# The state scan of a selective-scan mixer: 13 of 64 input products on ScalarE and GpSimd, convolutions summed in PSUM, seams and head in a new order

## The chip, the cores and the metric

The kernel runs on one core of a Trainium2 chip. Five engines share the work: TensorE (PE, with weight loads as PEld), VectorE (DVE), ScalarE (ACT), GpSimd (POOL) and SyncE (SP, which here only issues DMAs). Each has its own instruction stream; semaphores order them against each other. The metric is the device time of one execution in microseconds (us), as the median of the runs.

## The reference, cut to what matters

The model has two layers on an image x of shape (2, 256, 64, 64). The first layer is an area attention and an LSTM; they are not touched. The second layer begins with "the mixers", and ends with a mixture of experts, which is not touched either. The mixers take a normalised x and add to each of five groups of channels something else: 128 channels pass through, three groups of 32 channels get a depthwise convolution (3x3, 1x11, 11x1), and the last 32 channels get a selective scan over the 4096 pixels of an image:

```python
o_hw = _dwconv2d(x_hw, w_hw, b_hw, [(1, 1), (1, 1)])
o_w = _dwconv2d(x_w_, w_w, b_w, [(0, 0), (5, 5)])
o_h = _dwconv2d(x_h_, w_h, b_h, [(5, 5), (0, 0)])
o_m = _mamba(x_mb, ...)
...
# _mamba, with D_INNER = 64 and D_STATE = 16
u = jax.nn.silu(causal_conv1d(xm) + conv1d_b)
delta = jax.nn.softplus(jnp.einsum('blr,dr->bld', dt, dt_proj_w) + dt_proj_b)
A = -jnp.exp(A_log)
dA = jnp.exp(delta[..., None] * A)
dBu = delta[..., None] * Bm[:, :, None, :] * u[..., None]
def step(h, inputs):
    dA_t, dBu_t, C_t = inputs
    h = h * dA_t + dBu_t
    y = jnp.sum(h * C_t[:, None, :], axis=-1)
    return (h, y)
...
y = y + u * D
y = y * jax.nn.silu(z)
out = jnp.einsum('bld,cd->blc', y, out_proj_w)
...
x = x + _L1_conv_ref(_ln_c(x), ...)
```

## The kernel before, in words

Two images times 64 inner channels fill the 128 partitions. The 4096 pixels are cut into four parts of 1024 columns, and each part is scanned for each of the 16 states: 64 steps in all, each on a 128x1024 tile. All of this is in the method `run`, under a manual schedule: the order in which the program text emits instructions is the order on each engine, and the framework adds only the semaphores.

One step (function `state`, with what the main loop emits around it) does this for part i and state n:
- `spread` (L1775): two matmuls in bf16 lay row n of B over all partitions, into a PSUM tile bn of two banks. It is emitted one step ahead.
- `decay` (L1770): ScalarE makes da = exp(delta * a_n), two steps ahead.
- the product (L1783): VectorE multiplies bn, in PSUM, by du = delta * u, in SBUF, in place.
- the scan (L1786): VectorE runs h = da * h + bn along the columns, da from SBUF and bn from PSUM, to hs in SBUF. hs has two buffers.
- `carry` (L1792): ScalarE keeps the last column for the next part.
- cs (L1793): GpSimd multiplies hs by the row of C, which a DMA (`bring`) has spread over the partitions two steps ahead.
- `add` (L1796): two steps later TensorE adds cs into yp, the PSUM tile of the part's sum over the states, by an identity matrix: four passes of f32. yp has one buffer of two banks. `skip` puts u * D into it first (at state 2 of a part).

Beside the steps, `beside` lists what else is done at which state, "early" ahead of the state's own instructions and "late" behind them:
- The next part's preparation: `line` (0), `line_out` (1), `inner` (half at 2, half at 3), `inner_out` with its Silu (4), `step_sizes` (5), `absolute` and `positive` (6), `exponent` (7), `logarithm` (8), then on GpSimd `lost`, `found`, `whole`, `times_u` and `b_third` (9 to 13, L1691, L1694, L1697, L1701 and L1656), which end in the next part's du, and the gate's Silu (13). Softplus is computed as max(v, 0) + ln(1 + exp(-|v|)), with a correction of the rounding of 1 + e, which needs the tiles e, top and wm.
- The end of the part before, the seam: `close` (L1807) multiplies yp by the gate on VectorE, behind state 1; `put` (L1818) projects it on TensorE into po, behind state 6; `put_out` (L1826) adds po to x on VectorE, ahead of state 7's product.
- The convolutions, in 14 pieces: band matrices multiply on TensorE into a PSUM bank "pc" or two; ScalarE copies each four channels to an SBUF tile `got` (L1454), and GpSimd adds them to x (L1456).

Banks of PSUM: bn takes four, yp two, and everything else shares the two banks with the tag "m".

Ahead of the scan stands the head (the first part's preparation, L1718 to L1752), with a pool of eight banks. There GpSimd does the remaining `add_norm`s (L1434), and VectorE and ScalarE share the softplus; `whole` is on VectorE, Ln reads 1 + e from wm, and the negative A (`a_neg`) is computed right after `inner_out`.

Of the kernel before, what the change touches and what calls it, by code (L numbers as in the profile page):

```python
# [10 lines left out]
F32 = mybir.dt.float32  # L11
# [1328 lines left out]
class Mixers:  # L1340
# [92 lines left out]
        part = self.sh.tok[:, w, :P]  # L1433
        eng.tensor_scalar(part, part, self.more[:, w : w + 1], self.less[:, w : w + 1], ALU.mult, ALU.add)  # L1434

    def convolutions(self, pool, ps):


        nc, xn, tok = self.tc.nc, self.xn, self.sh.tok
# [4 lines left out]
        def begin(at, n):  # L1444
            pc = bank("pc").rearrange("p (c w) -> p c w", w=WW)[:, :n]
            bias = self.b_conv[:, at : at + n].unsqueeze(2).to_broadcast([96, n, WW])
            nc.tensor.matmul(pc, self.ones, bias, start=True, stop=False, skip_group_check=True)
            return pc

        def end(at, pc):  # L1450

            for h in range(0, pc.shape[1], 4):
                got = pool.tile([P, 4, WW], F32, name="got", bufs=2)
                nc.scalar.copy(got, pc[:, h : h + 4])  # L1454
                to = tok[:, :, P + at + h : P + at + h + 4]
                nc.gpsimd.tensor_tensor(to, to, got.rearrange("p c w -> p w c"), ALU.add)  # L1456

        def fetch(name, at, n):
            t = pool.tile([P, 12 * WW], F32, name="band", bufs=2)[:, : n * WW]
# [15 lines left out]
        def turn(at):  # L1475
            pt = bank("pt").rearrange("p (i m) -> p i m", m=P)
            for c in range(8):
                h, i = divmod(c, 4)
                nc.tensor.matmul(
                    pt[64 * h : 64 * h + 64, i], xn[:, at + c, 1 : 1 + WW], self.sh.ident,  # L1480
                    start=True, stop=True, tile_position=(0, 64 * h),
                )
            turned = self.turned = pool.tile([P, 4, P], F32, name="turned")
            return lambda: nc.scalar.copy(turned, pt)

        def across(at, w):
# [57 lines left out]
    def run(self, left, check=None):  # L1544
# [5 lines left out]
        with ExitStack() as ctx:  # L1550
# [3 lines left out]
            ctx.enter_context(tc.manual_schedule())  # L1554
            nc.gpsimd.memset(self.carry, 0.0)
            psum, temps = [None], [pt]
            conv = self.convolutions(p1, lambda: psum[0])

            def bank(name):
                return psum[0].tile([P, 512], F32, name=name, tag="m")  # L1560
# [5 lines left out]
            def each_half(work):  # L1566
                for h in range(0, ML, 512):
                    work(slice(h, h + 512))
# [46 lines left out]
            def gate_out(now):  # L1615
                zs = now["zs"] = p1.tile([P, ML], F32, name="zs")
                each_half(lambda at: nc.scalar.activation(zs[:, at], now.pop(("pz", at.start)), AF.Silu))

            def inner(now, at):

# [5 lines left out]
            def inner_out(now):  # L1626
                u = now["u"] = p1.tile([P, ML], F32, name="u")
                each_half(
                    lambda at: nc.scalar.activation(u[:, at], now.pop(("pu", at.start)), AF.Silu, bias=sh.col("c1_b"))
                )  # L1630

            def b_and_c(now, at):

                pbc = now["pbc", at.start] = bank("pbc")
                nc.tensor.matmul(pbc, self.w_bc, now["u"][:, at], start=True, stop=True)
# [31 lines left out]
                    lambda at: nc.scalar.activation(e[:, at], now["pd", at.start], AF.Abs, bias=sh.col("dt_b"))  # L1667
                )

            def positive(now, at, apart):  # L1670
                pd = now.pop(("pd", at.start))
                if apart:
                    nc.vector.tensor_scalar(now["top"][:, at], pd, sh.col("dt_b"), 0.0, ALU.add, ALU.max)
                else:
                    nc.scalar.activation(now["top"][:, at], pd, AF.Relu, bias=sh.col("dt_b"))

            def exponent(now, add=True):
                now["wm"] = temp("wm")
# [1 line left out]
                if add:  # L1680
                    nc.scalar.activation(now["wm"], now["e"], AF.Identity, bias=self.unit[:, 0:1])

            def logarithm(now, less=False):
                wm = now["wm"]
                now["delta"] = p2.tile([P, ML], F32, name="delta")
                nc.scalar.activation(now["delta"], wm, AF.Ln)
                if less:
                    nc.scalar.activation(wm, wm, AF.Identity, bias=self.unit[:, 1:2])

            def lost(now, eng):  # L1690
                eng.tensor_tensor(now["e"], now["e"], now["wm"], ALU.subtract)  # L1691
# [14 lines left out]
            with ExitStack() as own:  # L1706
                pool = own.enter_context(tc.tile_pool(name="m_pre", bufs=1))
                psum[0] = own.enter_context(tc.tile_pool(name="m_psum_m", bufs=8, space=PSUM))
                temps.append(own.enter_context(tc.tile_pool(name="m_pre_t", bufs=1)))
                before_line(first, None)  # L1710
                pieces = self.centre(pool, 0, CN, nc.vector)
                others = self.centre(pool, CN, GC, nc.gpsimd)
                next(conv)
                for _ in range(3):
                    next(pieces)

                idle = pool.tile([P, 1], F32, name="idle")
                nc.scalar.activation(idle, sh.eps5, AF.Silu)  # L1718
                next(conv)
                next(conv)  # L1720
                next(pieces)
                next(others)
                next(others)
                line(first, 0)
                line_out(first, True)
                each_half(lambda at: inner(first, at))
                inner_out(first)
                nc.scalar.activation(self.a_neg, sh.prm[:, COL["A_log"]], AF.Exp)
                nc.gpsimd.tensor_scalar(self.a_neg, self.a_neg, -1.0, None, ALU.mult)
                for _ in others:  # L1730
                    pass
                for w in left:
                    self.add_norm(nc.gpsimd, w)
                each_half(lambda at: step_sizes(first, at))
                absolute(first)
                exponent(first, False)
                each_half(lambda at: positive(first, at, True))
                nc.vector.tensor_scalar(first["wm"], first["e"], 1.0, None, ALU.add)
                logarithm(first)
                each_half(lambda at: b_and_c(first, at))  # L1740
                b_first(first, nc.vector.tensor_copy)
                each_half(lambda at: b_rest(first, at))
                nc.vector.tensor_scalar(first["wm"], first["wm"], -1.0, None, ALU.add)
                lost(first, nc.vector)
                b_second(first)
                c_out(first, 0)
                found(first, nc.vector)
                whole(first, nc.vector)
                b_third(first, nc.vector)
                nc.scalar.activation(idle, sh.eps5, AF.Exp)  # L1750
                times_u(first, nc.vector)
                next(conv)  # L1752
                temps.pop()

# [1 line left out]
            p3 = ctx.enter_context(tc.tile_pool(name="m_3", bufs=2))  # L1756
            p4 = ctx.enter_context(tc.tile_pool(name="m_4", bufs=4))
            steps = [(i, n) for i in range(len(parts)) for n in range(DS)]
            checks = iter(()) if check is None else check(ps)

            def bring(i, n):
# [8 lines left out]
                nc.scalar.activation(da, parts[i]["delta"], AF.Exp, scale=self.a_neg[:, n : n + 1])  # L1770

            def spread(i, n):
                bn = parts[i]["bn", n] = ps.tile([P, ML], F32, name="bn")
                each_half(
                    lambda at: nc.tensor.matmul(  # L1775
                        bn[:, at], self.spread[:, n], parts[i]["b"][:, at], start=True, stop=True
                    )
                )

            def state(i, n):  # L1780
                now, end = parts[i], (i, n) == steps[-1]
                bn = now.pop(("bn", n))
                nc.vector.tensor_tensor(bn, now["du"], bn, ALU.mult)  # L1783
                hs = p3.tile([P, ML], F32, name="hs")
                carry = self.carry[:, n : n + 1]
                nc.vector.tensor_tensor_scan(hs, now.pop(("da", n)), bn, carry, ALU.mult, ALU.add)  # L1786
                if end:
# [40 lines left out]
            def beside(i, n):  # L1828
# [7 lines left out]
                if n in pieces:  # L1836
                    late.append(lambda: next(conv, None))
                if i > 0:
                    early += {7: [lambda: put_out(i - 1, 0, CN)]}.get(n, [])
                    late += {6: [lambda: put(i - 1, 0, CN)]}.get(n, [])  # L1840
                early += {13: [lambda: gate_out(now)]}.get(n, [])
                late += {12: [lambda: each_half(lambda at: gate(now, at))]}.get(n, [])
                if new is None:
# [2 lines left out]
                    return early, late  # L1846
                early += {
                    1: [lambda: line_out(new, False)], 4: [lambda: inner_out(new)],
                    6: [lambda: absolute(new), lambda: each_half(lambda at: positive(new, at, False))],
                    7: [lambda: exponent(new)], 8: [lambda: logarithm(new, True)],  # L1850
                    9: [lambda: lost(new, nc.gpsimd)],
                    10: [lambda: b_first(new, nc.scalar.copy), lambda: c_out(new, i + 1)]
                    + [lambda: found(new, nc.gpsimd)],
# [4 lines left out]
                }.get(n, [])  # L1858
                late += {
                    0: [lambda: before_line(new, now["xl"]), lambda: line(new, i + 1)],  # L1860
                    2: [lambda: inner(new, slice(0, 512))], 3: [lambda: inner(new, slice(512, ML))],
                    5: [lambda: each_half(lambda at: step_sizes(new, at))],
                    9: [lambda: each_half(lambda at: b_and_c(new, at))],
                }.get(n, [])
# [7 lines left out]
            for m, (i, n) in enumerate(steps):  # L1872
# [6 lines left out]
                    work()  # L1879
                state(i, n)  # L1880
                if n == 2 and i > 0:

                    skip(i)
                if m > 1:
                    each_half(lambda at: add(*steps[m - 2], at))
                if n == 1 and i > 0:
                    each_half(lambda at: close(i - 1, at))
                if m + 2 < len(steps):
                    bring(*steps[m + 2])
                for work in late:  # L1890
# [703 lines left out]
```

## Time and profile before

| what | us |
| --- | --- |
| median of three runs (2777.76, 2790.4, 2782.73) | 2782.73 |
| the profiled execution | 2774.13 |
| its span | 2772.3 |
| head of the mixers, to the first product of the scan | 1779.0 to 1813.3 of the span |
| scan, from there to the end of the last scan | to 2074.0 |
| last close, projection and sum | to 2082.1 |
| VectorE busy between 1813 and 2079 | 238.4 of 266.0 |

The profile is that of one execution, 8.6 us shorter than the median; the part of its time outside the span is 1.8 us. Groups of instructions are listed by line, engine, operation and tiles ("out<-in"), with busy time and the mean of one in ns. Lists of waits name the instruction that waited, what ended the wait, and then the us in total, the number of waits and the longest. A line with three durations shows the shortest, the median and the longest of a group.

### The profile page before, as it was taken

What the parts mean: (1) busy time and instruction counts of PE and PEld (TensorE: products, weight loads), DVE (VectorE), ACT (ScalarE), POOL (GpSimd) and SP (SyncE); (2) the same over time, 40 slices, a digit from 0 to 9 for tenths busy, and PEclk for the clock granted to TensorE, in tenths of its full rate; (3) what the DMA queues carried; (4) which work ended last, traced back from release to release, by engine and by line L of the source; (5) the groups of instructions that cost most, each with busy time, mean ns of one, the idle gap of its engine ahead of it and who ended that gap; (6) DMA issues with size and microseconds to landing.
All of it is one profiled execution on the core that took longest, in us unless ns stands there. A gap on an engine that the chain in (4) does not pass through costs nothing.

```text
span 2772.3 us, 45729 instructions
## 1 busy us (share of the span) xinstructions
PE 2576.4 (93%) x17021; PEld 1476.3 (53%) x17021; DVE 1903.3 (69%) x3670; ACT 1555.2 (56%) x2661; POOL 1258.9 (45%) x1214
## 2 busy tenths in 40 slices
PE   7999999999999999999999999878885999999984
PEld 2232333333333333332899999734443788888873
DVE  4787888888888888878666767798888422221116
ACT  2567677676767667666654555676637422222223
POOL 1354645453544554532341000288762366666651
PEclk9999999999999999999999999989998999999995
DMA  3566676777676767774450000055544366666648
GB/s 138 99 124 132 131 140 130 138 135 137 131 138 132 138 130 138 133 135 85 153 208 24 24 24 7 13 130 153 148 122 169 113 225 228 231 229 223 224 172 355
DMA packets 108923, 390.78 MB, mean 141 GB/s; under 512 B 19912, under 2 KB 24400, under 8 KB 98960
## 3 DMA queue, kind: packets, MB, share of 16 engines
q0 software_dynamic: 69184, 284.61, 43.1%
q1 hardware_dynamic: 38272, 98.87, 11.1%
q10 hardware_dynamic: 1232, 4.25, 0.4%
q8 instruction: 137, 2.24, 0.3%
q14 instruction: 98, 0.80, 0.1%
HBM read 178.81 MB, written 49.09 MB: 82 GB/s over the span
## 4 chain that ended last, share of the span: by engine, by line
PE 80%; DVE 10%; issue 4%; ACT 2%; DMA 2%; POOL 1%; SPq 0%; DVEq 0%; ACTq 0%; POOLq 0%
PE ps L302 11%; PE ph L2338 9%; PE av_o L416 9%; PE py L2350 8%; PE po L170 8%; PE ps L403 8%; PE z L906 7%; PE z L865 6%; PE ps L398 3%; DVE hs L1786 2%; PE yp L1796 2%; PE po L182 1%; PE po L416 1%; DVE more L318 1%; PE px L2324 1%
## 5 line engine op out<-in xcount | busy, mean ns | idle before, releaser
L372 DVE SCALAR_TENSOR_TENSOR acc<-vh,w_pe,acc 128x1008 f32<-128x1008 f32 (+7 forms) x384 | 476.5, 1244 | 8.4
L635 POOL DMA_DIRECT2D sx<-ex x304 | 264.7, 958 | 451.0 <-ACT ex L410 193.4
L410 ACT ACTIVATE ex<-ps 128x1024 f32<-128x1024 f32 x384 | 372.9, 1025 | 116.6 <-issue 56.8
L318 DVE CUSTOM_DVE_ANT_0 more<-ps,more 128x512 f32<-128x512 f32 x480 | 303.0, 687 | 133.4 <-PE ps L302 127.9
L2340 ACT ACTIVATE act<-ph,wt 128x256 f32<-128x256 f32 x272 | 128.9, 474 | 388.7 <-PE ph L2338 382.5
L2326 DVE COPY xt<-px 128x512 f32<-128x512 f32 x68 | 47.0, 692 | 390.7 <-PE px L2324 390.7
L2338 PE MATMUL ph<-xt,wt 128*128 128x256 f32 x1088 | 288.0, 387 | 0.0
L403 PE MATMUL ps<-q,k 32*128 32x512 f32 x2048 | 286.3, 602 | 0.0
L2350 PE MATMUL py<-wt,act 128*128 128x256 f32 x1088 | 278.9, 379 | 0.0
L314 ACT ACTIVATE more<-ps 128x1024 f32<-128x1024 f32 x240 | 233.5, 1029 | 16.8 <-ACT sx L410 5.9
L630 POOL TENSOR_TENSOR sx<-sx,ex 128x1024 f32<-128x1024 f32 x60 | 141.3, 2355 | 210.1 <-PE ps L302 168.9
L2338 PEld LDWEIGHTS ph<-xt,wt 128*128 128x128 f32 x1088 | 188.6, 189 | 60.1 <-DVE xt L2326 21.5
L2350 PEld LDWEIGHTS py<-wt,act 128*128 128x128 f32 x1088 | 201.8, 190 | 24.4
L416 PE MATMUL av_o<-ex,vt 128*32 128x512 f32 x1536 | 205.6, 606 | 0.0
L2365 POOL DMA_INDIRECT results<-y,ri x136 | 138.1, 1015 | 131.9 <-DVE y L2358 100.9
L874 ACT ACTIVATE t<-z,bias 128x128 f32<-128x128 f32 x440 | 127.9, 362 | 118.5 <-PE z L906 118.5
L302 PE MATMUL ps<-k,q 32*128 32x512 f32 x1088 | 183.3, 639 | 1.9 <-DVE nm L308 1.4
L865 PE MATMUL z<-xs,u 128*128 128x128 f32 x1536 | 181.9, 275 | 0.0
L865 PEld LDWEIGHTS z<-xs,u 128*128 128x128 f32 x1536 | 176.5, 192 | 0.3 <-ACT xs L1049 0.3
L1793 POOL TENSOR_TENSOR cs<-hs,cs 128x1024 f32<-128x1024 f32 x63 | 148.9, 2365 | 54.3 <-DVE hs L1786 31.3
L906 PE MATMUL z<-xs,v 128*128 128x128 f32 x1400 | 167.0, 275 | 0.2
L906 PEld LDWEIGHTS z<-xs,v 128*128 128x128 f32 x1400 | 162.5, 192 | 1.4 <-DVE xs L925 0.5
(477 smaller groups left out, 4661.1 us busy)
## 6 DMA issues: line engine op xcount, KB each, us to landing
sx<-ex POOLq DMA_DIRECT2D x304, 512.0 KB, 5.1
cs<-c_rows SPq DMA_DIRECT2D x128, 256.0 KB
y<-results SPq DMA_DIRECT2D x32, 512.0 KB
x<-xrows SPq DMA_DIRECT2D x8, 1024.0 KB
rows<-xt SPq DMA_DIRECT2D x16, 512.0 KB
out_x<-res POOLq DMA_DIRECT2D x15, 512.0 KB, 7.0
xrows<-xn SPq DMA_DIRECT2D x24, 256.0 KB
u_rows<-xs SPq DMA_DIRECT2D x14, 384.0 KB
```

Source lines behind the costliest of these rows:

```text
L302: made.append(nc.tensor.matmul(tiles[h // 2][:, h % 2], qs[G, i // HM][head(h), i % HM * P : (i % HM + 1) * P], keys[head(h)], start=True, ...
L314: nc.scalar.activation(held["more"][j], tiles[j], AF.Relu)
L318: nc.vector.tensor_tensor_reduce(more, tiles[h // 2][:, h % 2], more, -1.0, 3.0e38, ALU.add, ALU.min, accum_out=nms[G][:, 0, h, i : i + 1],)
L372: mark(nc.vector.scalar_tensor_tensor(part, vh[:, c, 2 + r0 + dy : 2 + r1 + dy, w0 + dx : w1 + dx], w_pe[:, c, k : k + 1], part, ALU.mult, ...
L403: nc.tensor.matmul(tiles[h // 2][:, h % 2], k[head(h), m % HM * P : (m % HM + 1) * P], qs[G, n][head(h)], start=False, stop=True, tile_pos ...
L410: nc.scalar.activation(exs[i], tiles[i], AF.Exp, scale=HD**-0.5)
L416: nc.tensor.matmul(to[head(h)], lhs, exs[h // 2][:, h % 2], start=first, stop=last, tile_position=(0, HD * h))
L635: nc.gpsimd.dma_start(total[i], exs[i], accum_op=ALU.add)
L865: nc.tensor.matmul(z[c][g], u[:, k, c, g], xin[j][:, k], start=g == GATES[0] and k == 0, stop=False, skip_group_check=True,)
L906: nc.tensor.matmul(z[c][g], v[:, k, c, g], h[:, k], start=False, stop=k == 1, skip_group_check=True,)
L2338: nc.tensor.matmul(ph[:, hc], wt[:, at : at + P], xt[:, c], start=c == 0, stop=c == 1)
L2350: nc.tensor.matmul(py[:, j], act[:, hc, j * P : j * P + P], wt[:, at : at + C], start=hc == 0, stop=hc == NH - 1,)
```

## The change

- **13 products leave VectorE.** In parts 0 to 2 for states 4, 6 and 15, in the last part for 4, 6, 9 and 15: TensorE spreads the row of B into two "m" banks (`spread_apart`, behind state 2, 4, 7 or 13), ScalarE copies both to an SBUF tile (top, wm or e, as they are free), and GpSimd multiplies it by du (`times_du`, ahead of state 3, 5, 8 or 14). On GpSimd this product stands ahead of the cs that the step of state 3, 5, 8 or 14 emits. The scan of these states reads da and this tile, both in SBUF.
- **Convolutions.** TensorE adds x itself to pc by an identity matrix, and ScalarE copies the sum straight to x; GpSimd's adds and the `got` tiles are gone.
- **Tables.** ln(1 + e) takes its 1 as the activation's bias and no longer reads wm; after each Silu the set that has both exp and ln is loaded.
- **Seams.** `close` goes behind state 2, right ahead of `skip`; `put_out` goes behind state 7; both halves of `inner` stand at state 3; hs has three buffers; `turned` uses the tile e.
- **Head.** ScalarE does abs, exp, ln and max in a row; `whole` is on GpSimd, and the add_norms are GpSimd's last; 12 small matmuls ("busy") stand ahead of `inner`.

```diff
         def begin(at, n):
...
             nc.tensor.matmul(pc, self.ones, bias, start=True, stop=False, skip_group_check=True)
+            before = tok[:, :, P + at : P + at + n].rearrange("p w c -> p c w")
+            nc.tensor.matmul(pc, self.sh.ident, before, start=False, stop=False, skip_group_check=True)
             return pc
 
         def end(at, pc):
-            for h in range(0, pc.shape[1], 4):
-                got = pool.tile([P, 4, WW], F32, name="got", bufs=2)
-                nc.scalar.copy(got, pc[:, h : h + 4])
-                to = tok[:, :, P + at + h : P + at + h + 4]
-                nc.gpsimd.tensor_tensor(to, to, got.rearrange("p c w -> p w c"), ALU.add)
+            n = pc.shape[1]
+            nc.scalar.copy(tok[:, :, P + at : P + at + n], pc.rearrange("p c w -> p w c"))
...
-            turned = self.turned = pool.tile([P, 4, P], F32, name="turned")
+            turned = self.turned = temp("e")[:, : 4 * P].rearrange("p (i m) -> p i m", m=P)
...
             def gate_out(now):
...
+                if now is not parts[-1]:
+                    nc.scalar.preload_act_table_set("natural_log_exp_and_others")
             def inner_out(now):
...
+                nc.scalar.preload_act_table_set("natural_log_exp_and_others")
...
-                nc.scalar.activation(now["delta"], wm, AF.Ln)
+                nc.scalar.activation(now["delta"], of, AF.Ln, bias=self.unit[:, 0:1])
...
+                busy = bank("busy")
+                for _ in range(12):
+                    nc.tensor.matmul(
+                        busy[:, :256], self.ones, self.spread[:, 0:2].rearrange("p n d -> p (n d)"), start=True, stop=True
+                    )
...
+            APART = {2: 4, 4: 6, 13: 15}, {2: 4, 4: 6, 7: 9, 13: 15}
+            NAMES = {4: "top", 6: "wm", 9: "top", 15: "e"}, {4: "top", 6: "wm", 9: "top", 15: "wm"}
...
+            def spread_apart(i, n):
+                banks = parts[i]["apart", n] = [bank("ba") for _ in range(2)]
+                for h, to in enumerate(banks):
+                    nc.tensor.matmul(
+                        to, self.spread[:, n], parts[i]["b"][:, 512 * h : 512 * h + 512], start=True, stop=True
+                    )
+            def times_du(i, n, name):
+                now = parts[i]
+                bn = now["bn", n] = temp(name)
+                for h, part in enumerate(now.pop(("apart", n))):
+                    nc.scalar.copy(bn[:, 512 * h : 512 * h + 512], part)
+                nc.gpsimd.tensor_tensor(bn, now["du"], bn, ALU.mult)
...
-                nc.vector.tensor_tensor(bn, now["du"], bn, ALU.mult)
-                hs = p3.tile([P, ML], F32, name="hs")
+                if n not in APART[i == last].values():
+                    nc.vector.tensor_tensor(bn, now["du"], bn, ALU.mult)
+                hs = p3.tile([P, ML], F32, name="hs", bufs=3)
...
-                    early += {7: [lambda: put_out(i - 1, 0, CN)]}.get(n, [])
+                    late = {7: [lambda: put_out(i - 1, 0, CN)]}.get(n, []) + late
+                if n - 1 in apart:
+                    s = apart[n - 1]
+                    early.append(lambda: times_du(i, s, NAMES[i == last][s]))
+                if n in apart:
+                    late.append(lambda: spread_apart(i, apart[n]))
...
-                    2: [lambda: inner(new, slice(0, 512))], 3: [lambda: inner(new, slice(512, ML))],
+                    3: [lambda: each_half(lambda at: inner(new, at))],
...
                 if n == 2 and i > 0:
+                    each_half(lambda at: close(i - 1, at))
                     skip(i)
                 if m > 1:
                     each_half(lambda at: add(*steps[m - 2], at))
-                if n == 1 and i > 0:
-                    each_half(lambda at: close(i - 1, at))
```

The head, as it is emitted behind `inner_out`, before and after:

```python
# before
a_neg; rest of the centring; add_norms (GpSimd); step_sizes; absolute; exponent; positive (VectorE)
wm = 1 + e (VectorE); logarithm of wm; b_and_c; b_first; b_rest; wm - 1; lost; b_second; c_out
found; whole (VectorE); b_third; times_u; next(conv)
# after
step_sizes; b_and_c; absolute; exponent; logarithm of 1 + e; positive (ScalarE)
rest of the centring; b_first; b_rest; c_out; a_neg; b_second; whole (GpSimd)
wm = (1 + e) - 1 (VectorE); lost; found; b_third; times_u; add_norms (GpSimd); next(conv)
```

## The prediction

> **What bounds the kernel now.** I read the page's chain first, then the table by stretches for the mixers (1779 to 2082 us of the span), then groups, waits and releases in there.
>
> ```profile
> PE 80%; DVE 10%; issue 4%; ACT 2%; DMA 2%; POOL 1%; SPq 0%; DVEq 0%; ACTq 0%; POOLq 0%
> ```
>
> The whole kernel is TensorE's, but the change lies only in the mixers, where the chain passes through VectorE (DVE). Three stretches by engine (us; busy PE, PEld, DVE, ACT, POOL with counts; granted clock; DMA share; GB/s):
>
> ```profile
> 1779.00:1813.00 34.00, 14.28 (x148) 8.73 (x149) 26.39 (x47) 20.84 (x33) 20.80 (x20) 0.71 0.09 28
> 1813.00:2079.00 266.00, 230.62 (x1474) 110.72 (x1473) 238.42 (x152) 160.19 (x238) 202.58 (x110) 0.97 0.54 143
> ```
>
> In the scan DVE is busy 238.4 of 266.0 us, PE 230.6, GpSimd (POOL) 202.6: three engines are nearly full, so work taken from DVE meets the next one soon. The groups (busy us, mean ns) and DVE's waits (us, times, longest):
>
> ```profile
> L1786 DVE TENSOR_TENSOR_SCAN hs<-da,carry,bn 128x1024 f32<-128x1024 f32 x64 | 150.2, 2347 | 13.9 <-POOL cs L1793 5.6 <-ACT da L1770 1.0
> L1783 DVE TENSOR_TENSOR bn<-du,bn 128x1024 f32<-128x1024 f32 x64 | 77.5, 1211 | 0.9 <-PE bn L1775 0.6
> ```
>
> ```profile
> DVE zs L1807 <- PE yp L1796: 6.0, 3, 3.0
> DVE hs L1786 <- POOL cs L1793: 5.6, 6, 1.2
> DVE x L1826 <- PE po L1818: 4.4, 3, 1.6
> DVE hs L1786 <- ACT da L1770: 1.0, 2, 0.5
> ```
>
> A state is a product and a scan. In undisturbed rows the scan starts 1.34 us after its product and the next product 2.26 us after the scan: 3.60 a state, set by DVE. POOL's product with C (L1793) repeats every 2.31 when nothing holds it.
>
> **What goes.** 13 products leave DVE: 13 x 1.34 = 17.4. The close moves behind scan 2, put_out behind state 7, and hs gets a third buffer; the waits above have these as their places: 6.0 + 4.4 + 5.6 + 1.0 = 17.0. Together -34.4.
>
> **What comes: waits for GpSimd's product.** Its chain is spread (PE), two copies (ACT), product (POOL), and the scan waits for its end. Rows: spread .54 a pair; a 512-wide copy .54, so 1.1; product 2.31 (that of L1793). By hand, state by state:
> - State 4, parts 1 to 3. From the end Z of scan 2: close 1.2, then skip and the first add on the one yp bank, 3.7 (eight passes in the trace), then the spread: Z + 5.5; copies 6.5; product 8.85. DVE does close, product 3 and scan 3 by Z + 4.85. Wait 4.0, three times.
> - State 4, part 0: the first cs now stands behind whole and the add_norms, so it starts some 7.9 after the first product; with cs 0 to 2 and the product at 2.31 each that is 17.2 against 4 x 3.60 = 14.4: 2.9.
> - State 6: its spread is behind add 1 (1.72), inner (3.44), a spread, add 2 and itself: 13.5, copies to 15.15, POOL 17.55, against 14.95 on DVE: 2.6 in parts 1 and 2, 2.35 in the last, which has other work for PE; part 0, where POOL does cs 4 and the product in one state, 1.2.
> - State 15, parts 0 to 2. From scan 8's end POOL has cs 8 to 13, lost, found, whole, times_u and this product: 11 x 2.33, and b_third at 2.2: 27.9. DVE needs 22.8. Wait 5.1. The last part, without the next part's four: .65, and .7 at state 9.
>
> Sum 14.9 + 8.75 + 15.95 + .7 = 40.3. The scan would so be 5.9 longer than before, the removed 34.4 notwithstanding.
>
> **What comes: a lock between DVE and POOL.** In before every product and scan has one operand in PSUM. The 13 moved scans read da and the product both from SBUF. Two rows show what happens between POOL and a DVE operation with two operands in SBUF (min/median/max ns):
>
> ```profile
> L335 POOL TENSOR_TENSOR rest<-nm,parts x30: 215/1232/1279, 145.7 to 1268.4; 128x16 f32<-128x16 f32 x30
> L883 DVE TENSOR_TENSOR cell<-cell,hc x152: 291/292/614, 1341.4 to 1775.1; 128x128 f32<-128x128 f32 x152
> L1786 DVE TENSOR_TENSOR_SCAN hs<-da,carry,bn x64: 2346/2347/2348, 1814.6 to 2071.6; 128x1024 f32<-128x1024 f32 x64
> ```
>
> POOL's 16-element operation takes .215 alone and ends with DVE's L372 (both operands in SBUF, 1.24) when that runs. L883 grows from .291 to .53 beside POOL's L1043 of .57, and ends .14 after that. Today's scans never vary, with cs beside them all the time. The Trainium skill, "SBUF — State Buffer", section "Who interferes with whom", says the same as a rule: a DVE instruction with two SBUF inputs contends with a GpSimd instruction that reads SBUF, through a shared port that one holds for a whole instruction. The rows agree; no row of before has a scan with two such operands.
>
> On POOL the moved product stands ahead of the cs of the state before, which has long been ready when the product is late. In the trace POOL starts cs 32 to 61 ns before the operation ahead of it ends; DVE wakes 34 to 36 ns after a POOL operation it waits for. So POOL takes the port first and the scan then stands for all of cs: 2.36 (row: mean 2365). By place: state 4, 4 x 2.36 = 9.4; state 6, 2.4 in part 0 and .75 in the others (their spread, late for PE before, is covered by the earlier delay: product 6 then waits for cs 4, and cs 5 goes first), 4.65; state 15 in three parts 7.1; state 9 and the last 15, 2.4 each. Together 26. Ends: nothing (the scan doesn't lock) to 13 x 2.36 = 30.7; below nothing isn't possible, since no row shows contention to be lost. I take 26, as the nearest rows lock in both directions.
>
> **Convolutions, tables, head, tail.** 22 adds go from POOL (L1456, 855 ns, 18.5); one more matmul pair a group goes to PE, about .87 x 11 = 9.6, and ACT copies the same elements. POOL's share is spent again by 13 x 2.31 = 30, so this only pays for the products; PE's is inside the seams' gaps and counted at nothing, at most 9.6 if it falls where PE sets the end. A quarter fewer table loads (1.28 each) save ACT time that 160 of 266 us busy hides. In the Trainium skill, "ScalarE: Activation LUTs", section "What ACT_TABLE_LOAD costs", a switch also drains the pipeline and costs about 2.7; the trace has the next instruction at once behind the 1283 ns. By the page the head would gain 1.4 more for each load gone from its chain.
>
> Head: from u's end (1794.63) the chain becomes ident and busy matmuls (1.5), load 1.28, abs 1.25, exp 1.06, ln 1.06, relu 1.25, c_out 1.06, a_neg .22 and .27 (POOL), whole 2.36, found, b_third, times_u 1.36 each: 1810.6 for the first product instead of 1813.3: -2.7, with ends +1 (the port, between whole and DVE's additions) and -5 (no cold stretch). Tail +.2.
>
> **Sum.** -2.7 + .2 + (40.3 - 34.4) + 26 = +29.4, on the profiled execution's 2774.1: 2803.5. That execution is 8.6 below the median of the runs, 2782.7, which I add back: **2812**.
>
> **Rivals.**
> - *The scan doesn't lock, or DVE gets the port first.* Without the lock the sum is +3.4: 2786. With DVE first, cs is late by 2.35 instead, which costs .7 to 1.9 at state 6 and 2.35 at the end, about 7 in all: 2793. For: no row has a scan of that kind. Against: L335 and L883, and the 70 to 95 ns by which POOL is ahead. Either is within .5%.
> - *The products are in time (the faster side).* If the chains to states 4, 6 and 15 are shorter than my count by more than the waits (4.0, 2.6, 5.1), product s ends during scan s-1, DVE goes straight on and POOL's cs waits unseen. Half of the 40.3 gone and no lock: -2.7 + .2 - 34.4 + 20.2 = -16.7: 2766. All of it gone would be 2746, but PE would then be busy 240 of 229 us, so that can't be; PE's 240 bounds it near 2757. Against it: state 15 is a plain sum on POOL.
>
> **Chances.** Forecast .50 (2797 to 2822), the first rival .30 (2777 to 2797), the second .20 (2755 to 2770). Range 2766 to 2822: about .1 below, .06 above. Half a percent, 13.9 us, is what a measurement of this kernel tells from none: faster than 2768.8 .20, between .30, slower than 2796.6 .50.
>
> **What would show it.** Right: moved scans recorded at 4.6 us instead of 2.35 with cs beside them; a wait of DVE on POOL's product near 5 us before state 15 and 4 before state 4; no wait on zs or po. Wrong: all 64 scans at 2347; POOL idle before state 15's product; DVE's share of the scan above 90%. The first product at 1810.6 tests the head.

## The result, and the profile after

| | before | after |
| --- | --- | --- |
| median of five runs, us | 2782.73 | 2815.95 |
| ratio | | 1.0119, 95% interval 1.0101 to 1.0137 |
| span of the profiled execution | 2772.3 | 2813.7 |
| head: end of the last L1208 (ScalarE's normalising step, xn<-x) to the first product | 31.7 | 29.0 |
| scan: first product to the end of the last scan | 260.7 | 297.4 |
| tail, to the last put_out | 8.2 | 8.2 |
| from there to the span's end (not changed) | 690.1 | 698.8 |

The change costs 33 us. The three mixer rows give -2.7, +36.7 and 0, so +34.0; the part behind them is not touched and took 690 to 699 us in the profiles of this study; the part ahead of them, not touched either, ended between 1776.7 and 1786.2. That is why spans are not compared below, but the scan's length (read from the trace as in the table).

All scans of the kernel after, by what they read (count: shortest, median, longest in ns):

```profile
L1808 DVE TENSOR_TENSOR_SCAN hs<-da,carry,bn x51: 2345/2347/2348, 1810.6 to 2097.1; 128x1024 f32<-128x1024 f32 x51
L1808 DVE TENSOR_TENSOR_SCAN hs<-da,carry,top x5: 4416/4419/4482, 1824.9 to 2074.6; 128x1024 f32<-128x1024 f32 x5
L1808 DVE TENSOR_TENSOR_SCAN hs<-da,carry,wm x5: 4408/4418/4429, 1834.2 to 2102.3; 128x1024 f32<-128x1024 f32 x5
L1808 DVE TENSOR_TENSOR_SCAN hs<-da,carry,e x3: 4421/4421/4425, 1873.7 to 2026.5; 128x1024 f32<-128x1024 f32 x3
```

The 51 scans with bn in PSUM take what they took; the 13 with both operands in SBUF take 2.07 us more each, 27.0 in all. What happens at one of them, state 15 of part 2, on VectorE and then on GpSimd (start, duration, and the idle time before it):

```profile
2026.51 4.42 DVE L1808 TENSOR_TENSOR_SCAN hs<-da,carry,e 128x1024 f32<-128x1024 f32 x1 [5.18 <-POOL e L1799]
```

```profile
2024.13 2.34 POOL L1799 TENSOR_TENSOR e<-du,e 128x1024 f32<-128x1024 f32 x1
2026.44 2.34 POOL L1815 TENSOR_TENSOR cs<-hs,cs 128x1024 f32<-128x1024 f32 x1
```

The product ends at 2026.47. GpSimd has started cs of state 14 at 2026.44, VectorE starts the scan at 2026.51, .07 later, and the scan ends 2.15 after cs. VectorE's waits in the mixers:

```profile
DVE hs L1808 <- POOL top L1799: 20.1, 5, 7.0
DVE hs L1808 <- POOL e L1799: 15.5, 3, 5.2
DVE hs L1808 <- POOL wm L1799: 8.6, 5, 2.8
DVE zs L1829 <- PE yp L1818: 1.0, 1, 1.0
```

Inside the scan the waits on cs, da, po and yp are all gone (the 1.0 on yp is in the tail); 44.2 us of waits for GpSimd's product stand in their place. So for the scan: locks +27.0, new waits +44.2, products -17.4, removed waits -17.0: +36.8, against the measured 36.7. "Lock" is the prediction's word for a scan that stands while GpSimd's instruction runs.

### The profile page after: what moved, and what is told of

Read it like the earlier page. It is cut to its first block, busy times and chain, and to the rows that moved or that the text cites. A ratio compares the mean times of both kernels' runs of the same rounds, so it can differ in the third digit from the quotient of the medians.

```text
span 2813.7 us, 45794 instructions
## 1 busy us (share of the span) xinstructions
PE 2607.9 (93%) x17073; PEld 1488.4 (53%) x17073; DVE 1909.2 (68%) x3653; ACT 1557.6 (55%) x2676; POOL 1269.7 (45%) x1204
```

## The experiments

The theory: the scan grows by the lock and by waits for late products, and the other edits matter little. Rivals: the scan is slow by itself with two SBUF operands; or the new seams cost, not the products; or the moved products' chain is late for another reason than the prediction's. Scan lengths are from one profile each and carry no interval; undisturbed states, a product and a scan, repeat to .1 us over parts and kernels. Where a kernel has one run, its time says less: before's own runs went from 2775.7 to 2790.9.

**No moved product (no_apart).**

```diff
-            APART = {2: 4, 4: 6, 13: 15}, {2: 4, 4: 6, 7: 9, 13: 15}
+            APART = {}, {}
```

> The changed kernel with all 64 products left on VectorE, all its other edits kept. Lock theory with waits for GpSimd's product: the 13 scans' extra 27.0 us and the 44.2 us of waits before them go, 13 x 1.34 = 17.4 us of products come back, a few waits on cs return (up to 6): some 50 us under 2816, so 2760 to 2775, and all 64 scans at 2347 ns. Rival, the new seams (close behind state 2, a cold TensorE) are what costs: 2800 or more, with VectorE waiting in the seams.

Measured: 2781.84 us, ratio to before .9995 (.9983 to 1.0008); scan 268.7; all scans at 2347 ns. The 13 products carry the whole loss, and the "seams alone" rival falls. But the time is above the range: VectorE, freed of the waits for products, now waits for bn instead (23.6 us in the scan).

```profile
DVE bn L1805 <- PE bn L1782: 23.6, 17, 3.6
```

Without the products, the rest of the change is worth nothing as it stands: the scan is 8.1 us longer than before and the head 2.2 shorter, and the time is that of before. Of the 8.1 us, 4.2 go with the old seams (seams_old), 1.5 more with the old convolutions and two hs buffers, and 2.3 stay (both_old).

**The lock taken away, everything else kept (da_psum).** ScalarE writes da of a moved state to the PSUM tile that its bn would have had:

```diff
+                if n in APART[i == last].values():
+                    da = parts[i]["da", n] = ps.tile([P, ML], F32, name="bn")
+                else:
                     da = parts[i]["da", n] = p3.tile([P, ML], F32, name="da", bufs=3)
...
                 if n in APART[i == last].values():
+                    decay(i, n)
                     return
```

(For those states `decay` runs one step later than for the others, in `spread`'s place.)

> The changed kernel, but for the 13 moved states ScalarE writes da to a PSUM tile (the one that bn would have had), so that their scans read one operand from PSUM and one from SBUF; GpSimd's products and their order stay. Lock theory: these scans go from 4.42 back to 2.35 us with cs beside them, some 27 us less, with 2 to 6 of it lost again to longer waits at state 6: 2789 to 2795. Rival, a scan is slow next to any GpSimd product or the cost is the waits alone: scans stay above 4 us, 2810 or more.

Measured: 2798.52 us, ratio to before 1.0058 (1.0039 to 1.0078); scan 277.4, 20.0 less than after. The moved scans:

```profile
L1812 DVE TENSOR_TENSOR_SCAN hs<-bn,carry,top x5: 2349/2350/2351, 1826.7 to 2060.4; 128x1024 f32<-128x1024 f32 x5
L1812 DVE TENSOR_TENSOR_SCAN hs<-bn,carry,wm x5: 2349/2349/2350, 1835.2 to 2085.2; 128x1024 f32<-128x1024 f32 x5
L1812 DVE TENSOR_TENSOR_SCAN hs<-bn,carry,e x3: 2349/2349/2350, 1872.6 to 2016.2; 128x1024 f32<-128x1024 f32 x3
```

One operand moved from SBUF to PSUM takes the whole 2.07 us off, with GpSimd's products where they were and cs still started .07 to .09 ahead of each of these scans. That settles the mechanism of the duration. The gain in the scan is 20 and not 27 (18 with the tail, which is 2.0 longer), and the time 3.5 us above the range, since waits that the lock had covered come out:

```profile
DVE hs L1812 <- POOL top L1803: 18.1, 5, 5.6
DVE hs L1812 <- POOL wm L1803: 16.0, 5, 3.9
DVE hs L1812 <- POOL e L1803: 15.1, 3, 5.2
```

At state 6 the wait rises from 1.3, 1.3, 1.3 and 1.8 in parts 0 to 3 to 2.7, 3.9, 3.8 and 3.4; GpSimd now stands idle for 1.3 to 2.5 us ahead of product 6, waiting for ScalarE's copies. In parts 1 and 2 these start 1.8 us after their spread has ended: ScalarE is busy with a table load and two da's, one of them the da that this run makes a step later. So a part of what the lock seems not to be worth is this run's own doing.

**The order of the two changed (dve_first).** cs of the state before is emitted behind the moved scan and made to wait for it:

```diff
-                nc.vector.tensor_tensor_scan(hs, now.pop(("da", n)), bn, carry, ALU.mult, ALU.add)
+                scan = nc.vector.tensor_tensor_scan(hs, now.pop(("da", n)), bn, carry, ALU.mult, ALU.add)
+                if held:
+                    to, h = held.pop()
+                    late_cs = nc.gpsimd.tensor_tensor(to, h, to, ALU.mult)
+                    tc.add_manual_dep(late_cs.ins, scan.ins.name, behind, reason="behind the scan")
...
+                if n + 1 in APART[i == last].values():
+                    held.append((now["c", n], hs))
+                    return
                 nc.gpsimd.tensor_tensor(now["c", n], hs, now["c", n], ALU.mult)
```

> The changed kernel, but cs of the state before a moved one starts only when the moved scan has ended; nothing else is changed. Lock theory: the 13 scans take 2.35 us since GpSimd stands still beside them, and GpSimd is late by 2.35 instead; by the prediction's count the lock then costs 7 rather than 27: 2793 to 2800. Rival, a scan with both operands in SBUF is slow by itself: it stays at 4.4 us and the time rises over 2816.

Measured: 2808.27 us (one run), scan 283.4. The scans with both operands in SBUF take 2.35 us when GpSimd stands still:

```profile
L1810 DVE TENSOR_TENSOR_SCAN hs<-da,carry,top x5: 2350/2350/2351, 1829.4 to 2069.6; 128x1024 f32<-128x1024 f32 x5
L1810 DVE TENSOR_TENSOR_SCAN hs<-da,carry,wm x5: 2350/2351/2354, 1838.9 to 2094.7; 128x1024 f32<-128x1024 f32 x5
```

So they are not slow by themselves. The scan stage gains 14, not the 20 of the expectation, and the time is 8 us above its range: the late cs comes back as a wait of 3.6 to 3.7 at state 6 of every part (1.3 to 1.8 in after), as waits for bn (6.5), and in the tail, 13.5 us instead of 8.2, as a wait of 4.2 for yp. So who goes first is worth 8.6 us of scan and tail here, against the prediction's 19 us between the two cases.

**Two SBUF operands without a GpSimd product (sbuf_product).** As no_apart, but VectorE writes the 13 products to top, wm and e:

```diff
                 if n not in APART[i == last].values():
-                    nc.vector.tensor_tensor(bn, now["du"], bn, ALU.mult)
+                    name = NAMES[i == last].get(n) if i == last or n != 9 else None
+                    to = temp(name) if name is not None else bn
+                    nc.vector.tensor_tensor(to, now["du"], bn, ALU.mult)
+                    bn = to
```

> As no_apart (every product on VectorE), but the product of the same 13 states is written to an SBUF tile, so that these scans read both operands from SBUF; GpSimd does only cs and the next part's preparation. Lock theory: cs of the state before started 1.3 us ahead of the scan, so most of these scans take 2.35 + 1.0 = 3.3 to 3.5 us, more where GpSimd works back to back (up to 4.4): 13 to 20 us above no_apart. Rival, the scan is slow by itself with two SBUF operands: all 13 at 4.42, 27 above. Rival, no lock: all at 2.35, no difference.

Measured: 2784.79 us (one run), scan 272.2.

```profile
L1811 DVE TENSOR_TENSOR_SCAN hs<-da,carry,top x5: 2350/2700/3396, 1821.9 to 2050.4; 128x1024 f32<-128x1024 f32 x5
L1811 DVE TENSOR_TENSOR_SCAN hs<-da,carry,wm x5: 3225/3396/3411, 1830.1 to 2075.1; 128x1024 f32<-128x1024 f32 x5
L1811 DVE TENSOR_TENSOR_SCAN hs<-da,carry,e x3: 3733/3750/3754, 1864.8 to 2004.0; 128x1024 f32<-128x1024 f32 x3
```

The duration follows how much of GpSimd's cs is left when the scan starts: nothing where cs had ended (2350), about 1.0 where it had begun 1.1 to 1.2 earlier (3396), 1.4 at state 15. There GpSimd works back to back, and the next cs shows the other side of the lock:

```profile
1866.34 4.35 POOL L1818 TENSOR_TENSOR cs<-hs,cs 128x1024 f32<-128x1024 f32 x1
```

```profile
1864.79 3.73 DVE L1811 TENSOR_TENSOR_SCAN hs<-da,carry,e 128x1024 f32<-128x1024 f32 x1
```

The scan of state 15 starts at 1864.79, beside a cs that ends at 1866.37, and ends 2.15 us after that, at 1868.52; the second cs, started at 1866.34, ends 2.17 us after the scan and takes 4.35 us instead of 2.36. So the three went one after the other. The scans are 11.7 us longer together, yet the stage only 3.5 and the tail 2.4: most of the rest fills waits for bn that no_apart had anyway (16.1 us instead of 23.6). The duration was foreseen; its price, 13 to 20 us, was not.

**The close back behind state 1 (close_early).**

```diff
-                    each_half(lambda at: close(i - 1, at))
                     skip(i)
                 if m > 1:
                     each_half(lambda at: add(*steps[m - 2], at))
+                if n == 1 and i > 0:
+                    each_half(lambda at: close(i - 1, at))
```

> The changed kernel with the close back behind state 1, all else kept. If the wait before state 4 comes from the chain that the close starts behind scan 2 (close, skip and first add on a TensorE that had stood idle and runs at a lower clock, spread, copies, product), that wait falls from 7.0, 6.1 and 5.6 us in parts 1 to 3 to 2 or less, skip's matmuls keep the full clock, and the close waits 1.4 to 3.0 for yp again: mixers 6 to 12 us shorter, 2804 to 2810. Rival, GpSimd or ScalarE sets that wait: it stays above 5 us, 2814 to 2820. The 13 scans stay at 4.4 us in either case.

Measured: 2798.34 us (one run), 6 below the range; scan 283.1, 14.3 less than after. The wait before state 4 falls from 7.0, 6.1 and 5.6 to 1.25, 1.25 and 1.25, and the wait of the close for yp that was expected does not return. In after, GpSimd and ScalarE stand idle for 5.5 us and more ahead of these products, until TensorE's spread, so neither of them sets the wait. TensorE's rows at that place in part 1, first after, then close_early:

```profile
1890.02 3.78 PE L1818 MATMUL yp<-u,w_skip 128*128 128x512 f32 x4 [4.17 <-DVE zs L1829]
1893.60 3.19 PE L1818 MATMUL yp<-cs,ident 128*128 128x512 f32 x4
```

```profile
1885.13 1.98 PE L1818 MATMUL yp<-u,w_skip 128*128 128x512 f32 x4 [0.57 <-DVE zs L1829]
1886.95 1.88 PE L1818 MATMUL yp<-cs,ident 128*128 128x512 f32 x4
```

In after, TensorE stands idle for 4.17 us ahead of skip, and then does the same eight passes in 6.8 us instead of 3.7 (parts 2 and 3: gaps of 4.17 and 3.94, passes of 5.9 and 5.4). Four stretches of after around it, with the granted clock in the column before the last two:

```profile
1884.00:1890.00 6.00, 0.60 (x2) 0.11 (x2) 5.87 (x6) 4.28 (x7) 3.82 (x5) 0.95 0.35 89
1890.00:1894.00 4.00, 3.98 (x5) 1.85 (x6) 3.45 (x2) 0.07 (x1) 1.28 (x1) 0.50 0.00 0
1894.00:1898.00 4.00, 4.00 (x9) 1.55 (x8) 0.00 (x0) 0.96 (x3) 0.00 (x0) 0.72 0.00 0
1898.00:1902.00 4.00, 4.00 (x11) 1.71 (x10) 1.43 (x1) 2.51 (x4) 3.81 (x2) 1.00 0.80 235
```

The clock is .50 right behind the gap and back at 1.00 within eight us. The Trainium skill, "TensorE: Matmul & The Clock Gate", section "What's actually happening", gives half speed after an idle window of about 3.4 us, and full speed after one that was busy; the gap of 4.17 and the rows agree. A gap need not be that long here: in no_apart one of 2.82 at the same place was followed by .50 too (1881.70 to 1885.70), and the eight passes took 6.7. So the close behind scan 2 costs twice: TensorE waits for it, and works slowly after it.

**The other edits (seams_old, both_old).** seams_old is no_apart with the seams of before:

```diff
+                    early += {7: [lambda: put_out(i - 1, 0, CN)]}.get(n, [])
-                    late = {7: [lambda: put_out(i - 1, 0, CN)]}.get(n, []) + late
...
+                    2: [lambda: inner(new, slice(0, 512))], 3: [lambda: inner(new, slice(512, ML))],
-                    3: [lambda: each_half(lambda at: inner(new, at))],
...
-                    each_half(lambda at: close(i - 1, at))
                     skip(i)
...
+                if n == 1 and i > 0:
+                    each_half(lambda at: close(i - 1, at))
```

> As no_apart, with the seams of the kernel before (close behind state 1, put_out ahead of state 7, inner half at 2 and half at 3); the new convolutions, tables, head and the third hs buffer stay. If the late close delays the next spreads on TensorE, VectorE's waits for bn behind scans 3 and 4 of parts 1 to 3 (12 us in no_apart) go, and waits for yp and po of some 8 us return: 2 to 6 us below no_apart, 2776 to 2780. Rival, TensorE is late from the convolutions' identity matmuls: the waits for bn stay and the time is that of no_apart or above, 2782 to 2790.

Measured: 2786.33 us, ratio 1.0015 (1.0002 to 1.0028), scan 264.5, 4.2 less than no_apart. The time lies in the rival's range, the waits go as the theory said: from the end of the last L1208 the mixers are 4.8 us shorter than no_apart's in the profile, while the medians are 4.5 apart the other way. The two kernels ran in different rounds, their runs spread over 11 and 13 us, and the intervals of their ratios to before overlap, so the medians show no clear difference. What can be said is that the stage's wait for bn falls from 23.6 to 4.1 and waits for yp and po take most of its place (8.5 and 7.8 in the scan, the rest of these lines in the tail):

```profile
DVE x L1848 <- PE po L1840: 10.4, 5, 4.6
DVE zs L1829 <- PE yp L1818: 9.6, 5, 4.2
DVE bn L1805 <- PE bn L1782: 4.1, 6, 1.3
```

both_old also has before's convolutions and two hs buffers, so that only head and tables are new:

```diff
-            before = tok[:, :, P + at : P + at + n].rearrange("p w c -> p c w")
-            nc.tensor.matmul(pc, self.sh.ident, before, start=False, stop=False, skip_group_check=True)
...
-            nc.scalar.copy(tok[:, :, P + at : P + at + n], pc.rearrange("p c w -> p w c"))
+            for h in range(0, pc.shape[1], 4):
+                got = pool.tile([P, 4, WW], F32, name="got", bufs=2)
...
-                hs = p3.tile([P, ML], F32, name="hs", bufs=3)
+                hs = p3.tile([P, ML], F32, name="hs", bufs=2)
```

> As seams_old, with the convolutions of the kernel before as well (GpSimd's adds) and two hs buffers: of the change only the head and the table sets are left. Scan as long as before (260 to 262 us from the first product to the last scan's end), first product at 1806 to 1808 us instead of 1813: 5 to 7 us below before, 2775 to 2778. Rival, the head's gain is lost in the first states, where cs waits for the add_norms: within 2 us of before.

Measured: 2777.87 us, ratio .9990 (.9978 to 1.0001), scan 263.0, head 29.5. The head's 2.2 us are there, the scan is 2.3 longer in this profile (a wait of 2.7 for bn at the start of the last part), and the time is just not clear of before. The convolutions in PSUM with a third hs buffer gain nothing: the scan is 264.5 with them, 263.0 without. The medians, of the same round, stand further apart, 2786.33 and 2777.87; the mixers of the two profiles differ by .4 us, and where the other 8 us lie is open.

**The 13 products alone (only_apart).** before with `spread_apart`, `times_du` and the two tables, nothing else.

> The kernel before with the 13 products moved and nothing else. Theory: locks of some 2.07 x 13 = 27 us and waits for GpSimd's products (state 15 some 6 to 8 us in three parts, since the convolutions' adds stay on GpSimd; states 4 and 6 some 2 to 4 each) against 17.4 us of products: 25 to 40 us above before, 2808 to 2822, so that this part alone carries the whole loss of the change. Rival, the loss needs the new seams as well: under 2795.

Measured: 2815.34 us (one run), scan 291.2, 30.6 above before, with the 13 scans at 4.42. The products alone make the whole loss. Their waits are others than in after: 1.2 at state 4, 2.5 at state 6, 4.6 at state 15 (3.7 in the last part), and 1.2 at state 9.

**Without state 15 (no_15).**

```diff
-            APART = {2: 4, 4: 6, 13: 15}, {2: 4, 4: 6, 7: 9, 13: 15}
+            APART = {2: 4, 4: 6}, {2: 4, 4: 6, 7: 9}
```

> The changed kernel without the moved product of state 15 (nine moved products are left). If its wait is GpSimd's sum of work behind scan 8, waits of 5.2, 5.2, 5.2 and 2.8 us and four locks of 2.07 go, and four products of 1.34 come back: scan 297.4 - 18.4 - 8.3 + 5.4 = 276 us, time about 2795; up to 5 us of it may return as waits of the scans on cs or of the next part's start. Rival, the seam is full for another reason (du of the next part, TensorE): VectorE waits there all the same, scan over 287 us, 2805 or more.

Measured: 2802.76 us (one run, with before at 2790.20 beside it), scan 282.4, 14.9 less than after; 6 us more than the 276 expected (the expectation allowed for up to 5) came back; waits for bn of up to 1.9 us appear at the first states of each next part (9 us together). GpSimd works from 1845.8 to 1875.9 in after with no gap over .1 us, so the 5.2 us before state 15 are its sum of work.

**Lock and late close both gone (da_psum_early).** da_psum's edit on close_early.

> close_early with da of the 13 moved states in PSUM: both the lock and the late close are gone, the waits for GpSimd's products stay. Theory: scan of the mixers 283.1 - 27 us of locks, with 3 to 8 us given back where product 6 and 15 now stand open: 259 to 264 us, so about what it is without any moved product (264.5 with the same convolutions); time 2774 to 2782. Rival, something else of the moved products holds VectorE: over 268 us, 2784 or more.

Measured: 2789.41 us (one run), scan 268.8: 14.2 less than close_early, where 19 to 24 were expected. Scan and time both lie in the rival's range, 5 and 7 us above the theory's. The waits grow as the locks go: 1.8 to 2.1 at state 4 (1.25), 2.8 to 3.7 at state 6 (1.3 to 1.8), at state 15 of parts 0 to 2 they stay at 4.8 to 5.2. Waits for the products make 9 of the 12 us that VectorE stands idle more than in close_early, waits for yp 1.6; so the rival's cause, something else that holds VectorE, has little for it, but the theory's size was wrong again: 27 us of locks were worth 14 here. As in da_psum, ScalarE makes these da's a step later, ahead of the copies.

**Few products, in time, without the lock (few_early).** both_old with da_psum's edit and

```diff
+            APART = {}, {1: 4}, {1: 4}, {2: 5, 7: 10}
```

so that a product stands one cs earlier in GpSimd's queue (ahead of the cs of state s-2).

> both_old (new head and tables, old seams and convolutions) with four products on GpSimd, their da in PSUM (no lock), each queued on GpSimd one cs earlier than in the change, at states where it has time: state 4 in parts 1 and 2, states 5 and 10 in the last. Theory: no wait for the product, so each saves 1.34 us: scan 257 to 259 us instead of 263.0, some 5 us under both_old: 2771 to 2774. Rival, two hs buffers or the two shared banks give it back as waits: 2776 to 2780.

Measured: 2775.42 us, ratio to before .9980 (.9967 to .9993): a little faster than before, by .2%, and faster than the change by 1.4%. The intervals of few_early and both_old overlap, so how much of the .2% is the four products' and how much the head's can't be told from the times. The four scans:

```profile
L1813 DVE TENSOR_TENSOR_SCAN hs<-bn,carry,top x3: 2324/2326/2349, 1891.2 to 2028.3; 128x1024 f32<-128x1024 f32 x3
L1813 DVE TENSOR_TENSOR_SCAN hs<-bn,carry,wm x1: 2345/2345/2345, 2049.1 to 2049.1; 128x1024 f32<-128x1024 f32 x1
```

Not one of them waits for its product. But of 5.4 us of products, the scan shows 1.2 (261.8 against 263.0): the time comes back as longer waits for po (2.5, 2.5 and 1.9 instead of 1.6, 1.6 and 1.2) and for yp. That is the rival of its expectation in the cause, and a time between the two.

| kernel | scan, us | tail, us | median, us |
| --- | --- | --- | --- |
| before | 260.7 | 8.2 | 2782.73 |
| after | 297.4 | 8.2 | 2815.95 |
| only_apart | 291.2 | 8.5 | 2815.34 |
| dve_first | 283.4 | 13.5 | 2808.27 |
| close_early | 283.1 | 8.3 | 2798.34 |
| no_15 | 282.4 | 8.3 | 2802.76 |
| da_psum | 277.4 | 10.1 | 2798.52 |
| sbuf_product | 272.2 | 10.2 | 2784.79 |
| da_psum_early | 268.8 | 8.7 | 2789.41 |
| no_apart | 268.7 | 7.7 | 2781.84 |
| seams_old | 264.5 | 7.7 | 2786.33 |
| both_old | 263.0 | 8.3 | 2777.87 |
| few_early | 261.8 | 7.7 | 2775.42 |

The times come from several rounds, in which before's median was 2781.6 to 2782.7 (beside no_15, one run of 2790.2).

## Why the prediction was right, step by step

The forecast, 2812 us, was right in sign and size, and the runs show its mechanism, locks and late products; the time is 2815.95. That the size came so close is in part luck: errors of single waits cancel (below), and the two terms are not independent, as the sum had them. Without the lock it gave 2786 and da_psum measured 2798.5; with VectorE first it gave 2793 and dve_first measured 2808.3. More waits come out when the locks go than the sum had: 49.2 us in da_psum against 40.3, a part of them da_psum's own.

- *The lock, +26.* 27.0 us more in the 13 scans. The order was as forecast: GpSimd's cs starts .03 to .08 ahead of the scan. The scan takes 4.42 and not 4.6: in the rows above it ends 2.15 after cs. What the lock costs the stage seems to be less: taking it away gave 20.0 (da_psum) and 14.2 (da_psum_early), though these runs also delay ScalarE's copies.
- *Waits for the products, 40.3.* 44.2. State 15 in parts 0 to 2 was exact (5.2 each against 5.1, a sum on GpSimd). State 4 in parts 1 to 3 was mis-sized: 7.0, 6.1 and 5.6 against 4.0 each, 6.8 us in all. The term that failed is "skip and the first add, 3.7 (eight passes in the trace)": this duration is from a TensorE that came from work; behind the idle gaps of 4.17, 4.17 and 3.94 us that the late close makes, it was 6.8, 5.9 and 5.4, 7.0 more in all. State 4 of part 0 was 1.2 against 2.9 (the first cs began 4.9 and not 7.9 after the first product), and the last state 15 2.8 against .65 (GpSimd is idle for 2.5 us ahead of that product; the spread comes late). State 6 was 1.3 in three parts and 1.8 in the last, 5.8 in all against 8.75; the forecast had wait and lock together at 13.4 there, and they were 14.0.
- *Removed, -34.4.* 13 products, and the waits on cs, da, po and yp are all gone from the scan. What no_apart showed and the prediction did not consider: with the products back on VectorE, it waits 23.6 us for bn, and all but 4.1 of that goes with the old seams (seams_old). In the change .8 us of it shows; VectorE waits for the products instead.
- *Convolutions at nothing.* seams_old against both_old: 264.5 and 263.0, so nothing gained in the scan and 1.5 lost; the medians, 8.5 apart, leave the price open.
- *Head, -2.7.* 31.7 to 29.0 from the end of the last L1208. The first product came at 1809.3 instead of 1810.6 because the stage began 1.3 earlier in this execution. Table loads from the last L1208 to the last put_out went from 24 to 16, a third fewer and not a quarter.
- *Rivals.* "The products are in time": all 13 scans waited for theirs, by .16 at state 9 and by 1.2 or more at the others; "no lock, or VectorE first" is excluded by the 4.42 us rows.

Left open: why the median of seams_old is above those of no_apart and both_old, although its mixers are 4.8 us shorter than the one's and only .4 longer than the other's. The parts ahead of and behind the mixers differ by up to 9.5 us between profiles, and nothing here was tried on them.

## What to carry to other kernels

Before moving an operand from PSUM to SBUF, look at what the other of VectorE and GpSimd does at that moment: with two operands in SBUF a VectorE scan stood for what was left of GpSimd's instruction, and with one of them in PSUM it didn't. A product that is handed to another engine must be queued so early that it ends before its user is free; in few_early, with four products queued one cs earlier at chosen states, none was waited for. And where three engines are nearly full, a saved microsecond becomes a wait for the next one: of 5.4 us taken from VectorE in time and without the lock, the stage kept 1.2.

## What the runs showed of the hardware

- The scan with both operands in SBUF runs at its normal 2.35 us when GpSimd is idle (dve_first) and 4.42 us when GpSimd's 2.35 us multiplication starts just ahead of it. ScalarE's da took 1.11 us to PSUM and 1.14 to SBUF (da_psum).
- When GpSimd's product releases a scan, GpSimd's own next instruction is first: cs started 30 to 80 ns ahead of the scan at all 13 places of after.
- TensorE's clock went to .50 of full speed behind gaps of 4.17 us (after) and 2.82 us (no_apart), and eight f32 passes took 6.8 and 6.7 instead of 3.7 us.
